# Four gated cross-attention layers on one core: the order of a step's products in layers 0 and 1, and the place of the first experts' additions

## The chip, the cores and the metric

The kernel runs on one core of one Trainium2 chip. The metric is the device time of one execution in microseconds. A core has a tensor engine (PE, with its weight loads listed as PEld), a vector engine (DVE), a scalar engine (ACT), GpSimd (POOL) and a queue engine (SP) that here issues most of the DMAs. Each engine works through its own instructions in order and waits on semaphores for what others make. Matrix products land in PSUM[...].

## What is computed

Input x is 32 batch elements of 100 tokens of width 128; the context has 1444 positions per element. Four layers follow one another, each a gated attention over the context and a gated feed-forward part. The change touches layers 0 and 1:

```python
x = x + tanh(g_xattn[0]) * L0_xattn(layernorm(x), ctx, ctx, ...)   # 16 heads of 8, projections, biases
x = x + tanh(g_ffn[0])   * L0_ffn(layernorm(x), ...)               # shared expert + 8 routed ones, top 2
x = x + tanh(g_xattn[1]) * L1_xattn(ctx, ctx, layernorm(x), mask, W_v, W_o)   # 16 heads, masked by key
x = x + tanh(g_ffn[1])   * L1_ffn(layernorm(x), ...)               # 32 experts, top 4
# layers 2 and 3 follow

def attention_core(q, k, v):                    # of each head
    scores = einsum('bhqd,bhkd->bhqk', q, k) * scale
    return einsum('bhqk,bhkd->bhqd', softmax(scores), v)
```

In the feed-forward part of layer 0 each token's row goes to two experts. Their two results come back weighted and are added to x with the gate of that part. Layer normalization of x stands ahead of each part, so the mean and variance of a token's row are needed after every addition to x.

## The kernel before

**Attention of layers 0 and 1** is `heads_attention` (L273). Layer 1 runs it with `keyed=True`, which the trace shows by its lines (L481, L489, L626 with a bias `kb`). Scores are made twice. By query, queries on the partitions: `query_scores` (L561, product at L574), from three-term bf16 splits of k and q that are laid out over the partitions by a round trip through DRAM (`kd`, `qd`); `query_max` (L586, at L595) takes their maxima on DVE. By key, keys on the partitions: `key_scores` (L551, at L556), from fp32 operands. To these `key_exp` (L605) adds the negative maxima by a product with ones (`oneb`, L611), and ACT takes the exponential out of PSUM (L626 in layer 1, L630 in layer 0). `values` (L633) multiplies the exponentials with the values: three of the four heads of a group at L641, the fourth at L646.

**Steps.** The loop at L785 counts steps g; a batch element takes NT = 12 of them. In one step four row groups c = 0 to 3 of 32 partitions are handled, as the pairs (0, 1) and (2, 3). Three batch elements are in flight: scores by query of element b in steps 12 b to 12 b + 11, scores by key and exponentials `lag` = 14 steps later, values one step after that. Within a step the engines' order is what the code writes down (`manual_schedule`, L784): the entries of `plan` that fall due, then the block at L798 to L818, then `maxima` in the last step of an element, then the entries of `tail` that fall due, then `values(..., False)`. The entries of `tail` make the next elements' keys and queries (`k_part`, `q_in`, `q_out`), the values' projection (`v_part`) and the output (`end_turn`, `end_back`, `end_out`); in layer 1 there is no projection of keys or values. The functions in `beside` add further entries to `tail`.

**Banks.** All PSUM tiles of the attention but the output come from one pool `ps` of seven banks, used in turn (L286, L287); a new tile waits until the readers of the tile that lay seven before it are done. A step takes eight (four `pse`, four `psc`) and one for each product of the tail. The block at L798 takes the two of psc 2 and 3 first, then pse 0 and 1, pse 2 and 3, psc 0 and 1.

**Terms.** `k_seen` (L476, layer 1: keys that the mask hides set to zero), `k_terms` (L491) and `q_terms` (L459) split k and q into bf16 terms. They run on POOL, with a cast by ACT between (`k_first` L484, or the copies in `k_part` and `q_out`). Ahead of step 0 there are 20 steps that prepare element 0 and begin with element 1.

**The experts' results.** At the end of `ffn0` (L1659 to L1671) eight groups of four batch elements are handled in a loop: SP loads y (both results of each token, `back` in DRAM), POOL adds the two (`ya`, L1667), DVE adds the sum with the gate to x (L1669), and `moments` (L190) takes mean and variance of the four rows' sets (L193, L194). Then layer 1's attention begins; it takes the reciprocal deviations of all 32 elements at once with `inv_sqrt` (L196; square root on ACT at L200) and norms an element in the step 13 ahead of its first. Its first loads on SP are the context (L354) and the mask (L356).

Of the kernel before, what the change touches and what calls it, by code (L numbers as in the profile page):

```python
# [16 lines left out]
B, S, D = 32, 100, 128  # L17
# [11 lines left out]
GB = 4  # L29
NG = B // GB  # L30
GT = GB * S
LN_EPS = 1e-5
# [28 lines left out]
class Model:  # L61
# [211 lines left out]
    def heads_attention(self, layer, w, scale, bq=None, bk=None, bv=None, bo=None, keyed=False, beside=()):  # L273
# [7 lines left out]
        nc, tc = self.nc, self.tc  # L281
        E = mybir.EngineType
        with ExitStack() as es:
            pool = lambda n, k, **kw: es.enter_context(tc.tile_pool(name=f"a{layer}_{n}", bufs=k, **kw))
            once, two, three, xp = pool("one", 1), pool("two", 2), pool("three", 3), pool("ex", 3)
            ps, pvp = pool("ps", 7, space=PSUM), pool("pv", 1, space=PSUM)  # L286
            bank = lambda n, dt=F32: ps.tile([P, 512 if dt == F32 else 1024], dt, name=n, tag="s")  # L287
            rstd = self.inv_sqrt(self.mv[:, :, 1], LN_EPS, "ln")
            gate = self.gate_x(layer)

            qm = once.tile([P, NSET, S], F32, name="qm")
# [55 lines left out]
            st = [{} for _ in range(B)]  # L347
# [93 lines left out]
            def q_out(b):  # L441
# [8 lines left out]
                if stacked:  # L450
# [5 lines left out]
                        scale=scale, **bias,  # L456
                    )

            def q_terms(b):  # L459
                r, qt, dram = st[b].pop("qr"), qts[b % 2], self.qd[b % 2]  # L460
                nc.gpsimd.tensor_tensor(r, r, qt[:, 0, 0, :], ALU.subtract)
                nc.gpsimd.tensor_copy(qt[:, 3, 0, :], r)
                nc.gpsimd.tensor_copy(qt[:, 1, 1, :], r)
                nc.gpsimd.tensor_copy(qt[:, 2, 1, :], r)
                nc.gpsimd.tensor_tensor(qt[:, 0, 1, :], r, qt[:, 3, 0, :], ALU.subtract)
                nc.sync.dma_start(
                    dram.rearrange("(p s) n -> p (s n)", s=4), qt.rearrange("p s v q -> p (s v q)")
                )
# [7 lines left out]
            def k_seen(b, i):  # L476

                at = slice(i * QTR, (i + 1) * QTR)
                t = st[b]
                t["kr", i] = two.tile([P, QTR], F32, name="kr")  # L480
                nc.gpsimd.tensor_scalar(t["kr", i], t["mi"][:, at], 0.0, 0.0, ALU.is_equal, ALU.is_equal)  # L481
                nc.gpsimd.tensor_tensor(t["kr", i], t["kr", i], t["k"][:, at], ALU.mult)

            def k_first(b, i):  # L484
                t = st[b]
# [3 lines left out]
                nc.scalar.copy(t["kt", h][:, 0, j * QTR : (j + 1) * QTR], t["kr", i])  # L489

            def k_terms(b, i):  # L491
                t = st[b]
                h, j = divmod(i, 2)
                kt = t["kt", h][:, :, j * QTR : (j + 1) * QTR]
                if keyed:
                    r = k = t.pop(("kr", i))
                else:
                    k = t["k"][:, i * QTR : (i + 1) * QTR]
                    r = two.tile([P, QTR], F32, name="kr")
                nc.gpsimd.tensor_tensor(r, k, kt[:, 0], ALU.subtract)  # L500
                nc.gpsimd.tensor_copy(kt[:, 1], r)
                nc.gpsimd.tensor_tensor(kt[:, 2], r, kt[:, 1], ALU.subtract)  # L502
# [281 lines left out]
            with tc.manual_schedule(engines={E.PE, E.DVE, E.Activation, E.Pool, E.SP}):  # L784
                for g in range(plan[0][0], NT * (B - 1) + end + 5):  # L785
                    def at(step):
                        b, r = divmod(g - step, NT)
                        return b if r == 0 and 0 <= b < B else None

                    for step, f in plan:  # L790
                        if (b := at(step)) is not None:
                            f(b)
                    def now(step):
                        b, t = divmod(g - step, NT)
                        return (b, t) if 0 <= b < B else None

                    keys, queries, products = now(lag), now(0), now(lag + 1)
                    if stacked:  # L798


                        if queries:
                            for c in (2, 3):
                                st[queries[0]]["psc", c] = bank("psc")
                        if keys:
                            key_scores(*keys, (0, 1))
                        if queries:
                            query_scores(*queries, (2, 3))
                            query_max(*queries, (2, 3))
                        if keys:
                            key_scores(*keys, (2, 3))  # L810
                            key_exp(*keys, (0, 1))
                        if queries:
                            query_scores(*queries, (0, 1))
                            query_max(*queries, (0, 1))
                        if keys:
                            key_exp(*keys, (2, 3))
                        if products:
                            values(*products, True)  # L818
                    for cs, others in () if stacked else (((0, 1), (2, 3)), ((2, 3), (0, 1))):
# [677 lines left out]
    def ffn0(self, w):  # L1497
# [4 lines left out]
        with ExitStack() as es:  # L1502
# [153 lines left out]
                    todo = e, i, h, out  # L1656
            down(*todo)

            for g in range(NG):  # L1659
                y = f2.tile([S, GB, K, D], F32, name="y")  # L1660
                i = nc.sync.dma_start(
                    y.rearrange("p b k d -> p b (k d)"),
                    self.back[g * GT * K : (g + 1) * GT * K].rearrange("(b p k) d -> p b (k d)", p=S, k=K),
                )
                self.after(i, back)
                ya = f2.tile([S, GB, D], F32, name="ya")
                nc.gpsimd.tensor_tensor(ya, y[:, :, 0, :], y[:, :, 1, :], ALU.add)  # L1667
                xs = self.x[:, g * GB : (g + 1) * GB, :]
                nc.vector.scalar_tensor_tensor(xs, ya, self.gate_f(0), xs, ALU.mult, ALU.add)  # L1669
                for b in range(g * GB, (g + 1) * GB):  # L1670
                    self.moments(b)  # L1671

    def ffn1(self, w):

# [338 lines left out]
def tile_gated_cross_attention_stack(ctx: ExitStack, tc: tile.TileContext, ins: dict, out: bass.AP):  # L2013
# [22 lines left out]
    with ExitStack() as ctx2:  # L2036
        later = []
        a, f = weights(1, {"q": sq, "t": sq, "o": sq}, {
            "gw": ("F1_gw", [P, 32], None),
            "sel128": ("sel128", [P, 16, P], None, BF16),  # L2040
            "w1": ("F1_w1", [P, 2048], None),
            "w3": ("F1_w3", [P, 2048], None),
            "w2": ("F1_w2", [P, 16, P], None),
            "b2": ("F1_b2", [P, P], None),
            "sw1": ("F1_sw1", sq, None),
            "sw3": ("F1_sw3", sq, None),
            "sw2": ("F1_sw2", sq, None),
        }, later)
        by_query = m.nc.values_load(
            m.by_query[0:1, 0:1], min_val=0, max_val=1, skip_runtime_bounds_check_because="it is a comparison's result"  # L2050
        )
        with tc.If(by_query == 0) as keyed:
            m.heads_attention(1, a, D ** -0.5, keyed=True, beside=[m.loads(later)])
        with keyed.Else():
            m.heads_attention(1, {**a, "k": a["q"], "v": a["q"]}, D ** -0.5, beside=[m.loads(later)])
        m.ffn1(f)
    with ExitStack() as ctx2:
        a, f = weights(2, {"q": sq, "k": sq, "v": sq}, {
# [120 lines left out]
```

## Time and profile before

| | us |
|---|---|
| median of three runs | 4278.3 (4276.38 to 4279.37) |
| the profiled execution, its own time | 4294.4 |
| its span, first to last instruction | 4292.6 |
| busy: PE / DVE / ACT / POOL | 3670.5 / 2845.1 / 2407.5 / 1706.5 |
| mean granted clock of PE | 0.955 |

The stages, from the trace: attention of layer 0 to about 1480, feed-forward of layer 0 to about 1796, a stretch to 1858 in which PE makes nine products in all, attention of layer 1 to about 3205, then the rest.

A row of the time line gives start and length in us, engine, line, operation, output and inputs, partitions x elements, how many instructions were merged, and in brackets how long the engine had been idle and what ended that. A row of a group gives busy time and mean length in ns, then the idle time of the engine ahead of it and who ended most of it. Matmuls overlap: the array works on several row groups at once, and an fp32 product shows as two passes, so each has two rows. Their ends are modelled.

### The profile page before, as it was taken

To read this page: it belongs to the slowest core of one execution; us is meant where nothing else is said; L and a number is where in the kernel's file an instruction comes from. 1 tells how busy PE (TensorE), PEld (TensorE's weight loads), DVE (VectorE), ACT (ScalarE), POOL (GpSimd) and SP (SyncE) were. 2 spreads that over 40 slices of the span, in tenths; PEclk is the share of its full clock that TensorE was granted. 3 is DMA by queue.
4 is the path that set the end of the run, shared out by engine and by line. 5 is a ranking of instruction groups with operands and counts; after the bars stand their busy time and mean duration, and the time that the engine had idled before them with its cause. 6 is when DMAs were issued, how large, how long until landed. Compare 5 with 4: busy or idle time off the path is not lost. (4 is left out here: it accounts for less than half of the span.)

```text
span 4292.6 us, 92353 instructions
## 1 busy us (share of the span) xinstructions
PE 3670.5 (86%) x36522; PEld 1991.4 (46%) x36522; DVE 2845.1 (66%) x6428; ACT 2407.5 (56%) x5274; POOL 1706.5 (40%) x2549
## 2 busy tenths in 40 slices
PE   6999999999999989668888888888887998886587
PEld 2444444444444445424444444444444556764354
DVE  5767767777777643357777777777748875553577
ACT  3666666666666642136666666676662324552474
POOL 5444444444444223465455454544500000113573
PEclk8999999999999989869999999999998999987799
DMA  5354344344343120244443343434310004541331
GB/s 171 126 163 146 119 142 127 106 138 125 112 138 120 61 71 16 71 172 169 150 161 138 139 148 134 162 136 142 134 64 8 1 1 181 199 167 37 115 114 36
DMA packets 286485, 500.06 MB, mean 116 GB/s; under 512 B 54993, under 2 KB 241967, under 8 KB 285258
## 3 DMA queue, kind: packets, MB, share of 16 engines
q1 hardware_dynamic: 275594, 475.26, 33.4%
q0 software_dynamic: 10432, 18.63, 1.4%
q8 instruction: 293, 4.80, 0.5%
q14 instruction: 166, 1.36, 0.1%
HBM read 360.24 MB, written 135.22 MB: 115 GB/s over the span
## 5 line engine op out<-in xcount | busy, mean ns | idle before, releaser
L595 DVE TENSOR_REDUCE mx<-psc 100x1 f32<-100x482 f32 (+1 forms) x3072 | 1824.6, 653 | 741.1 <-PE psc L574 509.4
L574 PE MATMUL psc<-ks,qs 32*100 32x482 bf16 (+1 forms) x6144 | 1184.9, 384 | 335.2 <-DVE mx L595 299.7
L556 PE MATMUL pse<-q,kt 32*128 32x400 f32 x6144 | 1034.5, 527 | 1.0 <-ACT maxt L672 1.0
L626 ACT ACTIVATE ex<-pse,kb 128x400 f32<-128x400 f32 (+1 forms) x1536 | 794.8, 591 | 339.1 <-PE psc L574 137.9
L630 ACT ACTIVATE ex<-pse 128x400 f32<-128x400 f32 (+1 forms) x1536 | 680.8, 502 | 372.9 <-PE pse L611 336.3
L574 PEld LDWEIGHTS <-qs 32*100 32x100 bf16 x6144 | 331.4, 120 | 749.7 <-issue 642.3
L556 PEld LDWEIGHTS pse<-q,kt 32*128 32x128 f32 x6144 | 522.7, 184 | 128.7 <-issue 68.1
L611 PE MATMUL pse<-maxt,oneb 32*128 32x400 bf16 x3072 | 513.8, 334 | 0.2
L661 POOL CAST mexp<-neg 100x16 bf16<-100x16 f32 x64 | 16.2, 253 | 718.7 <-DVE neg L657 454.5
L500 POOL TENSOR_TENSOR kr<-kt,kterm 128x361 f32<-128x361 f32 x128 | 108.3, 846 | 457.1 <-ACT kterm L531 455.3
L641 PE MATMUL pav<-ex,vn 128*32 128x300 f32 (+1 forms) x3072 | 277.2, 429 | 0.7 <-ACT oc L698 0.7
L641 PE MATMUL pav<-ex,v 128*32 128x300 f32 (+1 forms) x3072 | 275.1, 428 | 0.3 <-ACT oc L698 0.3
L502 POOL TENSOR_TENSOR kterm<-kr,kterm 128x361 bf16<-128x361 f32 x256 | 217.3, 849 | 20.7
L500 POOL TENSOR_TENSOR kr<-kr,kterm 128x361 f32<-128x361 f32 x128 | 108.3, 846 | 244.3 <-ACT kterm L489 213.9
L149 POOL DMA_INDIRECT sent<-rows_out,place x96 | 95.5, 995 | 251.6 <-DVE dn L1182 136.5
L1449 ACT ACTIVATE sl<-g,cols 128x400 f32<-128x400 f32 x136 | 80.7, 593 | 202.6 <-PE g L1440 149.8
L251 POOL TENSOR_SCALAR amo<-ami 100x361 bf16<-100x361 int32 x128 | 185.6, 1450 | 13.2 <-DMA ami<-in_mask 13.1
L481 POOL TENSOR_SCALAR kr<-mi 128x361 f32<-128x361 int32 x128 | 184.4, 1440 | 1.8 <-DMA mi<-in_mask 1.8
L611 PEld LDWEIGHTS <-oneb 32*128 32x128 bf16 x3072 | 149.7, 92 | 7.3 <-issue 1.0
L646 PE MATMUL pav<-ex,vn 128*32 128x100 f32 (+1 forms) x3072 | 149.2, 255 | 0.0
L646 PE MATMUL pav<-ex,v 128*32 128x100 f32 (+1 forms) x3072 | 143.5, 258 | 0.0
L522 PE MATMUL pk<-ct,w_A_k 128*128 128x361 f32 x256 | 118.4, 548 | 25.0 <-DMA ct<-in_ctxT 25.0
(491 smaller groups left out, 6011.9 us busy)
## 6 DMA issues: line engine op xcount, KB each, us to landing
ks<-kd SPq DMA_DIRECT2D x128, 722.0 KB
ct<-in_ctxT SPq DMA_DIRECT2D x96, 722.0 KB
kd<-kterm SPq DMA_DIRECT2D x128, 541.5 KB
vn<-in_ctxV SPq DMA_DIRECT2D x32, 1008.0 KB
cnat<-in_ctxN SPq DMA_DIRECT2D x32, 768.0 KB
kd<-kterm SPq DMA_DIRECT2D x128, 180.5 KB
kt<-in_ctxT SPq DMA_DIRECT2D x32, 722.0 KB
mi<-in_mask SPq DMA_DIRECT2D x32, 722.0 KB
```

The lines of the kernel that those rows point to most:

```text
L251: nc.gpsimd.tensor_scalar(t, now[h], 0.0, NEG, ALU.is_equal, ALU.mult)
L481: nc.gpsimd.tensor_scalar(t["kr", i], t["mi"][:, at], 0.0, 0.0, ALU.is_equal, ALU.is_equal)
L500: nc.gpsimd.tensor_tensor(r, k, kt[:, 0], ALU.subtract)
L502: nc.gpsimd.tensor_tensor(kt[:, 2], r, kt[:, 1], ALU.subtract)
L556: nc.tensor.matmul(s_["pse", c][:, : NSET * S], s_["k"][r, t * P : (t + 1) * P], s_["q"][r].rearrange("p s q -> p (s q)"), start=True, sto ...
L574: nc.tensor.matmul(t["psc", c][:S, : z - a], t["qs"][r, s, v, :], t["ks"][r, s, a:z], start=v == 0, stop=v == 1,)
L595: nc.vector.tensor_reduce(mx, src, AX.X, ALU.max)
L611: nc.tensor.matmul(pps[c][:, : NSET * S], oneb[r], s_["max"][r], start=False, stop=not by_query)
L626: nc.scalar.activation(ex[:kp, c], pps[c][:kp, : NSET * S], AF.Exp, bias=s_["kb"][:kp, t : t + 1])
L630: nc.scalar.activation(ex[:kp, c], pps[c][:kp, : NSET * S], AF.Exp)
L641: nc.tensor.matmul(s_["out"][32 * c : 32 * c + 32, S : NSET * S], s_["v"][:kp, t, o + 16 : o + 48], ex[:kp, c, S:], start=t == 0, stop=t = ...
L646: nc.tensor.matmul(s_["out"][32 * c : 32 * c + 32, :S], s_["v"][:kp, t, o : o + 32], ex[:kp, c, :S], start=False, stop=t == NT - 1, skip_g ...
```

## The change

It has three parts.

1. In the block of a step the products with the values (three heads) and the last exponentials now stand ahead of the scores by query of the pair (0, 1) and their maxima. The two banks of psc 2 and 3 are no longer taken first.
2. `ffn0` adds only group 0 of the experts' results. Groups 1 to 7 are loaded and added beside layer 1's attention: loads in steps 1, 5, 9, 13, 17, 21, 25, additions three steps later. The sum on POOL goes; DVE makes two gated additions instead. Layer 1 takes the reciprocal deviations of the first four elements ahead of its loop, and the other 28 in step 30.
3. For batch element 0 of layers 0 and 1 `q_terms`, `k_seen` and `k_terms` run on DVE, not on POOL.

```diff
-            rstd = self.inv_sqrt(self.mv[:, :, 1], LN_EPS, "ln")
+            if layer == 1:
+                rstd = once.tile([S, B], F32, name="rstd")
+                def scales(bs):
+                    v = rstd[:, bs]
+                    nc.vector.tensor_scalar(v, self.mv[:, bs, 1], 1.0, LN_EPS, ALU.mult, ALU.add)
+                    nc.scalar.activation(v, v, AF.Sqrt)
+                    nc.vector.reciprocal(v, v)
+                scales(slice(0, GB))
+                self.rest_of_scales = lambda: scales(slice(GB, B))
+            else:
+                rstd = self.inv_sqrt(self.mv[:, :, 1], LN_EPS, "ln")
...
+            terms_engine = lambda b: nc.gpsimd if b else nc.vector
             def q_terms(b):
-                nc.gpsimd.tensor_tensor(r, r, qt[:, 0, 0, :], ALU.subtract)
+                e = terms_engine(b)
+                e.tensor_tensor(r, r, qt[:, 0, 0, :], ALU.subtract)
...
                     if stacked:
-                        if queries:
-                            for c in (2, 3):
-                                st[queries[0]]["psc", c] = bank("psc")
                         if keys:
                             key_scores(*keys, (0, 1))
                         if queries:
                             query_scores(*queries, (2, 3))
                             query_max(*queries, (2, 3))
                         if keys:
                             key_scores(*keys, (2, 3))
                             key_exp(*keys, (0, 1))
-                        if queries:
-                            query_scores(*queries, (0, 1))
-                            query_max(*queries, (0, 1))
                         if keys:
                             key_exp(*keys, (2, 3))
                         if products:
                             values(*products, True)
+                        if queries:
+                            query_scores(*queries, (0, 1))
+                            query_max(*queries, (0, 1))
...
-            for g in range(NG):
-                y = f2.tile([S, GB, K, D], F32, name="y")
-                i = nc.sync.dma_start(y..., self.back[g * GT * K : (g + 1) * GT * K]...)
-                self.after(i, back)
-                ya = f2.tile([S, GB, D], F32, name="ya")
-                nc.gpsimd.tensor_tensor(ya, y[:, :, 0, :], y[:, :, 1, :], ALU.add)
-                xs = self.x[:, g * GB : (g + 1) * GB, :]
-                nc.vector.scalar_tensor_tensor(xs, ya, self.gate_f(0), xs, ALU.mult, ALU.add)
-                for b in range(g * GB, (g + 1) * GB):
-                    self.moments(b)
+            self.sent_back = back
+            self.results0_add(self.results0(f2, 0), 0)
...
+    def results0_add(self, y, g):
+        xs = self.x[:, g * GB : (g + 1) * GB, :]
+        for k in range(2):
+            self.nc.vector.scalar_tensor_tensor(xs, y[:, :, k, :], self.gate_f(0), xs, ALU.mult, ALU.add)
+        for b in range(g * GB, (g + 1) * GB):
+            self.moments(b)
+
+    def results_beside(self, es):
+        pool = es.enter_context(self.tc.tile_pool(name="cb", bufs=1))
+        now = {}
+        def load(b, i):
+            g = 1 + 3 * b + i
+            if g < NG:
+                now[g] = self.results0(pool, g)
+        def add(b, i):
+            g = 1 + 3 * b + i
+            if g < NG:
+                self.results0_add(now.pop(g), g)
+        def scales(b):
+            if b == 2:
+                self.rest_of_scales()
+        return [(s + d, lambda b, i=i, f=f: f(b, i)) for i, s in enumerate((1, 5, 9))
+                for d, f in ((0, load), (3, add))] + [(6, scales)]
...
-            m.heads_attention(1, a, D ** -0.5, keyed=True, beside=[m.loads(later)])
+            m.heads_attention(1, a, D ** -0.5, keyed=True, beside=[m.results_beside, m.loads(later)])
```

`results0` holds the load that stood in the loop, for one group. The same substitution of `terms_engine` is made in `k_seen` and `k_terms`; the other branch of layer 1 (by query) gets `results_beside` too, and does not run here.

More of the change, by code (lines that the diff above doesn't have):

```diff
@@ L457, in q_out @@
                     )
+            terms_engine = lambda b: nc.gpsimd if b else nc.vector
             def q_terms(b):
                 r, qt, dram = st[b].pop("qr"), qts[b % 2], self.qd[b % 2]
-                nc.gpsimd.tensor_tensor(r, r, qt[:, 0, 0, :], ALU.subtract)
[L462 to L465, printed above, removed]
+                e = terms_engine(b)
+                e.tensor_tensor(r, r, qt[:, 0, 0, :], ALU.subtract)
+                e.tensor_copy(qt[:, 3, 0, :], r)
+                e.tensor_copy(qt[:, 1, 1, :], r)
+                e.tensor_copy(qt[:, 2, 1, :], r)
+                e.tensor_tensor(qt[:, 0, 1, :], r, qt[:, 3, 0, :], ALU.subtract)
                 nc.sync.dma_start(
@@ L478, in k_seen @@
                 at = slice(i * QTR, (i + 1) * QTR)
-                t = st[b]
+                t, e = st[b], terms_engine(b)
                 t["kr", i] = two.tile([P, QTR], F32, name="kr")
-                nc.gpsimd.tensor_scalar(t["kr", i], t["mi"][:, at], 0.0, 0.0, ALU.is_equal, ALU.is_equal)
-                nc.gpsimd.tensor_tensor(t["kr", i], t["kr", i], t["k"][:, at], ALU.mult)
+                e.tensor_scalar(t["kr", i], t["mi"][:, at], 0.0, 0.0, ALU.is_equal, ALU.is_equal)
+                e.tensor_tensor(t["kr", i], t["kr", i], t["k"][:, at], ALU.mult)
             def k_first(b, i):
@@ L491, in k_terms @@
             def k_terms(b, i):
-                t = st[b]
+                t, e = st[b], terms_engine(b)
                 h, j = divmod(i, 2)
@@ L499, in k_terms @@
                     r = two.tile([P, QTR], F32, name="kr")
-                nc.gpsimd.tensor_tensor(r, k, kt[:, 0], ALU.subtract)
-                nc.gpsimd.tensor_copy(kt[:, 1], r)
-                nc.gpsimd.tensor_tensor(kt[:, 2], r, kt[:, 1], ALU.subtract)
+                e.tensor_tensor(r, k, kt[:, 0], ALU.subtract)
+                e.tensor_copy(kt[:, 1], r)
+                e.tensor_tensor(kt[:, 2], r, kt[:, 1], ALU.subtract)
                 if j:
@@ L1657, in ffn0, with results0 @@
             down(*todo)
-            for g in range(NG):
-                y = f2.tile([S, GB, K, D], F32, name="y")
[L1661 to L1664, printed above, removed]
-                self.after(i, back)
-                ya = f2.tile([S, GB, D], F32, name="ya")
-                nc.gpsimd.tensor_tensor(ya, y[:, :, 0, :], y[:, :, 1, :], ALU.add)
-                xs = self.x[:, g * GB : (g + 1) * GB, :]
-                nc.vector.scalar_tensor_tensor(xs, ya, self.gate_f(0), xs, ALU.mult, ALU.add)
-                for b in range(g * GB, (g + 1) * GB):
-                    self.moments(b)
+            self.sent_back = back
+            self.results0_add(self.results0(f2, 0), 0)
+    def results0(self, pool, g):
+        nc, K = self.nc, 2
+        y = pool.tile([S, GB, K, D], F32, name="y")
+        i = nc.sync.dma_start(
+            y.rearrange("p b k d -> p b (k d)"),
+            self.back[g * GT * K : (g + 1) * GT * K].rearrange("(b p k) d -> p b (k d)", p=S, k=K),
+        )
+        self.after(i, self.sent_back)
+        return y
+    def results0_add(self, y, g):
[20 more added lines that the diff above has]
+                for d, f in ((0, load), (3, add))] + [(6, scales)]
     def ffn1(self, w):
@@ L2052, in tile_gated_cross_attention_stack @@
         with tc.If(by_query == 0) as keyed:
-            m.heads_attention(1, a, D ** -0.5, keyed=True, beside=[m.loads(later)])
+            m.heads_attention(1, a, D ** -0.5, keyed=True, beside=[m.results_beside, m.loads(later)])
         with keyed.Else():
-            m.heads_attention(1, {**a, "k": a["q"], "v": a["q"]}, D ** -0.5, beside=[m.loads(later)])
+            m.heads_attention(1, {**a, "k": a["q"], "v": a["q"]}, D ** -0.5, beside=[m.results_beside, m.loads(later)])
         m.ffn1(f)
```

## The prediction

> **What bounds the kernel now.** I read the page's slices and costliest groups first, then the busy time by stage, then single steps in the order of time. Two stages fill most of the span, the attentions of layers 0 and 1:
>
> ```profile
> 84.00:1480.00 1396.00, 1265.93 (x14579) 636.60 (x14573) 993.17 (x1888) 883.43 (x2002) 610.36 (x812) 1.00 0.41 128
> ...
> 1796.00:1858.00 62.00, 2.03 (x9) 1.27 (x13) 18.08 (x80) 3.73 (x11) 39.45 (x53) 0.50 0.50 161
> 1858.00:1890.00 32.00, 31.04 (x147) 10.62 (x147) 30.75 (x56) 3.48 (x12) 19.19 (x31) 0.50 0.57 205
> 1890.00:3205.00 1315.00, 1141.75 (x14956) 575.43 (x14955) 962.00 (x1828) 912.97 (x1965) 620.03 (x941) 0.99 0.40 138
> ```
>
> (Stretch and length, then busy time of PE, PEld, DVE, ACT and POOL, granted clock, DMA share.) In both attentions no engine but PE is near full, and PE's figure counts overlapping row groups, so it is no proof either. The groups name the wait:
>
> ```profile
> L595 DVE TENSOR_REDUCE mx<-psc 100x1 f32<-100x482 f32 (+1 forms) x3072 | 1824.6, 653 | 741.1 <-PE psc L574 509.4
> L574 PE MATMUL psc<-ks,qs 32*100 32x482 bf16 (+1 forms) x6144 | 1184.9, 384 | 335.2 <-DVE mx L595 299.7
> ```
>
> PE waits for the maxima and the maxima for PE. One step of layer 0 with no tail work shows how:
>
> ```profile
> 1022.80 0.60 PE L556 MATMUL pse<-q,kt 32*128 32x400 f32 x2
> 1022.82 0.61 PE L574 MATMUL psc<-ks,qs 32*100 32x480 bf16 x4
> 1023.24 0.52 PE L556 MATMUL pse<-q,kt 32*128 32x400 f32 x4
> 1023.58 0.34 PE L611 MATMUL pse<-maxt,oneb 32*128 32x400 bf16 x2
> 1023.60 0.50 PE L556 MATMUL pse<-q,kt 32*128 32x400 f32 x2
> 1023.75 0.36 PE L574 MATMUL psc<-ks,qs 32*100 32x480 bf16 x1
> 1024.53 0.40 PE L574 MATMUL psc<-ks,qs 32*100 32x480 bf16 x2 [0.42 <-DVE mx L595]
> 1024.54 0.34 PE L611 MATMUL pse<-maxt,oneb 32*128 32x400 bf16 x2
> 1024.73 0.36 PE L574 MATMUL psc<-ks,qs 32*100 32x480 bf16 x1
> 1025.02 0.71 PE L641 MATMUL pav<-ex,v 128*32 128x300 f32 x8
> 1025.55 0.35 PE L646 MATMUL pav<-ex,v 128*32 128x100 f32 x8
> ```
>
> ```profile
> 1023.82 2.37 DVE L595 TENSOR_REDUCE mx<-psc 100x1 f32<-100x480 f32 x4 [1.59 <-PE psc L574]
> 1024.21 1.84 ACT L630 ACTIVATE ex<-pse 128x400 f32<-128x400 f32 x4 [0.59 <-PE pse L611]
> ```
>
> The step is 3.03 us (next one at 1025.83). At 1023.75 one score by query of the pair (0, 1) starts; its partner starts at 1024.53, 0.78 us later, 0.05 after the first maximum is done (1023.82 + 0.66). The cause is the ring of seven banks: a step takes eight, so the eighth, psc 1, gets the bank of this same step's psc 2. The wait stands in every step of both layers (683 in the list of waits). The reader is to see that PE's sequence behind it is late by 0.78 us.
>
> Between the two attentions PE is idle for 62 us:
>
> ```profile
> 1796.14 19.97 SPq L1661 DMA_DIRECT2D y<-back  x8
> ...
> 1823.45 0.36 SPq L356 DMA_DIRECT2D mi<-in_mask  x1
> ...
> 1827.77 1.46 POOL L481 TENSOR_SCALAR kr<-mi 128x361 f32<-128x361 int32 x1 [1.76 <-DMA mi<-in_mask]
> ...
> 1857.92 1.05 PE L574 MATMUL psc<-ks,qs 32*100 32x482 bf16 x8 [26.17 <-DMA qs<-qd]
> ```
>
> Eight loads and additions, then the first mask load (it takes memory the additions free), then POOL's terms.
>
> **Part 1, the new order in a step.** Nothing is added. Let B be the start of the second pair of scores by key (0.44 to 0.46 into a step). From rows of the step above: the product of oneb for pair (2, 3) follows at B + 0.67 (two passes of 0.336), the values 0.25 later (0.167 of streaming, 0.09 until the next shape), and take 0.53. Now psc 0, 1 follow them, second term 0.20 later, then 0.29 to the last values (1024.73 to 1025.02 shows it), then 0.28 to the next step. Here the Trainium skill speaks against the change: "TensorEngine Tiling (Array Packing)", section Tiling Modes, says that changing the tiling mode drains the engine and that different tiles work in parallel. The new order changes mode twice more per step (128x32 values, 32x128 scores, values) and takes psc 0, 1 out of the company of oneb (2, 3). The row for a change: 0.29 from psc to values where 482 columns stream in 0.20, so 0.09; values to a 128x128 product 0.64 against 0.53 without a change, so 0.11. By the rule alone the change costs about 0.2 in each of some 740 steps, near 150 us, plus 0.4 of lost company; by the rows these 0.6 are paid, but the 0.78 of waiting goes. PE alone: psc 0, 1 at B + 0.67 + 0.25 + 0.53 + 0.11 = B + 1.56, next step at B + 2.33.
>
> What is late next are banks of the next step. The eighth bank now comes from the same step's first exponential; that starts 0.95 after B (1024.21 after 1023.25) and ends at B + 1.50 in layer 0, before B + 1.56; with layer 1's 0.59 us exponentials at B + 1.60, 0.05 late. The next second pair takes the banks of the last exponential and of the first maximum of (0, 1). Exponentials, all four now back to back: last one ends at B + 0.95 + 3 x 0.475 + 0.50 + 0.05 = B + 2.93 in layer 0, B + 3.1 in layer 1. Maximum: it starts 0.44 after the second term, as single instructions show (1.73 and 2.17 into a step), ends 0.71 later: B + 1.76 + 1.15 = B + 2.91. So a plain step is 2.93 in layer 0 (3.03 now) and 3.09 in layer 1 (3.10 now).
>
> With tail work of 0.8 us or more on PE these banks are free by then, and the step is 2.33 + tail + 0.45 where it was 3.03 + tail: shorter by 0.25, and by a further 0.1 as the tail no longer pays the change from the values; I take 0.30. The phases of layer 0, twelve to a batch element: six with long tails (pk three times, pv, px with pv, pv with pa) -1.8; three plain -0.3; pk with pm, po -0.1 each; pq with pt 0, as DVE's q, now behind later maxima, holds pq's bank. Sum -2.3 of 45.75 measured; 31 elements: **-71 us**. Layer 1 has short tails: a tail of one bank moves the ring, so both maxima must end (B + 3.49) before the next second pair: px, pm, pa +0.2 together, po -0.1, the long pg -0.3, the short pg +0.3, plain ones -0.3 (one is 3.35 now). Sum -0.2 of 41.4: **-7 us**.
>
> **Part 2, the additions.** Removed from the gap: seven loads, seven POOL sums (1.26), seven DVE additions (0.75). The mask load then waits for group 0 alone: load landed 1800.5, two additions 1.47, so 1802.1 against 1823.45: -21.4. Added beside: seven times two additions of 0.72 and four bnst, mv pairs (1.1), 2.6 us on DVE. Three fall in steps 4, 8, 12, where DVE sets the pace (busy 30.75 of 32): +7.7. Four fall in full steps, behind the maxima; mx of the next step starts up to 2.5 late, and of that some 1.7 passes on: +7. The rest of the scales at step 30: DVE waits in order for ACT's square root with two table loads (1.28 each as at 1892.6): +3, with nothing of its kind in a full step; bounds 0 and 5. The loads on SP stand in front of key reads needed steps later; 0.3 us of issue, hidden. DMA is at 0.40.
>
> **Part 3, first terms on DVE.** In layer 1 POOL's chain is 1827.77 to 1850.5 for four parts and q's terms. DVE on 128x361 from SBUF is not in the trace; nearest row: the addition of 512 columns, 0.75, gives 0.53 by length; the casts lie between 0.2 and 0.5. A part becomes 3.1 with ACT's cast between, for 5.5: 12.4 + 1.9 for norm, q and terms; -8. But DVE is in order, and every part now waits there for ACT with norm behind it; bounds -11 and 0. In layer 0 terms stand ahead of the reciprocal and the norm that PE's third pk waits for (26.46), so the 0.9 saved per part is given back: 0, bounds -2 and +2. Part 2 and 3: -21.4 + 17.7 - 8 = **-12**.
>
> **Sum.** The profiled execution took 4294.4 (span 4292.6): 4294.4 - 71 - 7 - 12 = 4204. The median of the runs shown is 16 lower: **4188**.
>
> **Rivals.** (A) Late maxima. The first maximum of (2, 3) starts 0.75 after its second term (1.01 and 0.26 into a step). I put that down to the scores by key issued earlier and ending at 0.94. If 0.75 is the price from product to DVE, both maxima of (0, 1) end 0.32 later, at the end of the step and in front of the next second pair. Layer 1: +0.19 in five plain steps, +0.32 in six with short tails, 2.9; layer 0: 2.1 by the same count; 155 us over 31 elements: 4188 + 155 = 4343, slower. It decides from 0.44 + 0.32 x 90/155 = 0.62 us on. Against it: the maximum that started 0.44 after its own product. (B) Exponentials bind. Layer 0 gains nothing, as ACT's copies of pk and pv between the exponentials hold banks and the first exponential: 4278 - 19 = 4259. For it: ACT has 883 of 1396 and would be a closed chain in plain steps. Against: long tails leave it over 1 us. (C) Fuller gain: POOL or DVE work falls in the slack and the 0.11 comes back in all tails; layer 0 at -3.1, layer 1 at -1.0: -127 - 12, 4140. That the order doesn't change is excluded: the built program has psc 0, 1 behind the values, waiting on ACT.
>
> **Numbers.** My forecast 0.55 (4150 to 4225), B 0.17, C 0.11, A 0.17. Range 4140 to 4290: it takes in B and C and the near side of A. A measurement of this kernel tells 0.2% (8.6 us) from no change. Faster: 0.55 + 0.11 + 0.12 of B = 0.78, less 0.04 for a forecast that errs as a whole, 0.74; same 0.05; slower 0.21.
>
> **What would show it.** psc 0, 1 without a wait on mx; plain steps of 2.9 in layer 0 and 3.1 in layer 1, long ones 3.7; the maximum of psc 0 0.44 after its product (A wrong) or 0.75; the mask load of layer 1 near 1802 and first scores by query some 29 us sooner relative to the last scatter. Wrong if layer 1's steps exceed 3.3, or the granted clock falls below 0.99 in either attention.

## The result, and the profile after

The changed kernel takes 4303.2 us (median of five, 4296.7 to 4307.0), the kernel before 4279.4 (five, 4276.4 to 4282.2). The ratio is 1.0056, with a 95% interval of 1.0045 to 1.0067: it is slower by 24 us where 90 less were forecast, and lies outside the range. The profiled execution took 4303.2, its span is 4301.4, the mean granted clock 0.956.

Measured from one instruction to another in the two traces, the time went here (us):

| stretch | before | after | difference | forecast |
|---|---|---|---|---|
| start to the first score by query of layer 0 | 43.75 | 46.22 | +2.5 | 0 |
| layer 0, first score by key to last score by query | 1406.9 | 1391.8 | -15.2 | -71 |
| last product of its values to the experts' first product down | 184.0 | 172.1 | -11.8 | 0 |
| last scatter of results to the first score by query of layer 1 | 65.0 | 39.6 | -25.4 | -29.4 |
| from there to its first score by key | 32.0 | 38.1 | +6.1 | +7.7 |
| layer 1, first score by key to last score by query | 1277.2 | 1336.1 | +58.9 | +3 |
| all the rest | 1283.7 | 1277.5 | -6.2 | 0 |

The -11.8 is no gain of the change. The same stretch took 170.4 to 172.8 us in e1 to e8 below and 182.6 to 186.6 in e9 to e12, which ran on another chip. In the trace of before TensorE stops there from 1592 us on, for up to 4.1 us at a time, and its granted clock is 0.91 over 80 us where the changed kernel has 1.00. These 11.8 us are most of the 15 by which that execution lay above its median. So a difference of less than some 10 us between two profiles is used here only where it can be put to an instruction.

The groups of the changed kernel that answer to the two of before:

```profile
L612 DVE TENSOR_REDUCE mx<-psc 100x1 f32<-100x482 f32 (+1 forms) x3072 | 1870.3, 652 | 744.6 <-PE psc L591 682.0
...
L591 PE MATMUL psc<-ks,qs 32*100 32x482 bf16 (+1 forms) x6144 | 1021.9, 390 | 34.8 <-DMA qs<-qd 26.1
```

The wait that the change was read to remove is gone: TensorE's idle time ahead of scores by query fell from 335.2 to 34.8 us. A plain step without a stall (one with no product of the tail) is 2.88 us in both layers, and the maximum of psc 0 starts 0.40 after its second term. Yet the twelve steps of an element are only 0.49 us shorter in layer 0, by their medians, and 1.08 longer in layer 1. This is step 5 of an element of layer 0, where 4.34 us became 5.26 (the time line; the brackets hold the idle time before and what ended it):

```profile
1002.13 0.60 PE L573 MATMUL pse<-q,kt 32*128 32x400 f32 x2
...
1002.23 0.62 DVE L462 SCALAR_TENSOR_TENSOR q<-pq,cols,qm 128x400 f32<-128x400 f32 x1
...
1002.57 0.85 PE L573 MATMUL pse<-q,kt 32*128 32x400 f32 x4
...
1002.89 0.34 ACT L466 ACTIVATE qr<-pq,bqs 128x100 f32<-128x100 f32 x1 [1.38 <-DVE q L462]
...
1003.13 0.50 ACT L467 ACTIVATE qt<-pq,bqs 128x300 bf16<-128x300 f32 x1
...
1003.69 0.60 PE L573 MATMUL pse<-q,kt 32*128 32x400 f32 x1 [0.28 <-ACT qt L467]
```

Read it from the bottom. The fourth score by key starts 1.56 us into the step, where 0.46 is its place; it waits for the bank that pq, a tail product of step 4, had taken. Three readers hold that bank one after the other: VectorE's q, then ScalarE's two copies. VectorE's q was free to start only at 1002.23, behind the last maximum of the pair (0, 1), which now comes at the end of a step. ScalarE, which idled 1.38 us, waited for q. The chain is not new. This is the kernel before, in a step 5 that starts at 1010.92:

```profile
1010.29 0.63 DVE L449 SCALAR_TENSOR_TENSOR q<-pq,cols,qm 128x400 f32<-128x400 f32 x1
...
1010.95 0.34 ACT L453 ACTIVATE qr<-pq,bqs 128x100 f32<-128x100 f32 x1 [0.77 <-DVE q L449]
...
1011.19 0.50 ACT L454 ACTIVATE qt<-pq,bqs 128x300 bf16<-128x300 f32 x1
...
1011.75 0.18 PEld L556 LDWEIGHTS pse<-q,kt 32*128 32x128 f32 x1 [0.18 <-ACT qt L454]
```

There q starts 0.63 us ahead of the step and the copies end 0.77 into it; the fourth score by key waits for them too, until 0.83. Now q starts 0.10 into the step and the copies end at 1.50: both come 0.73 later. In the changed kernel every element shows the wait for q (the view of one line, L466, in both layers):

```profile
L466 ACT ACTIVATE qr<-pq,bqs x32: 343/343/345, 33.1 to 1410.3; 128x100 f32<-128x100 f32 x32
...
  DVE q L462: 46.5, 32
  DVE q L460: 36.8, 32
```

Why ScalarE may not read the bank beside VectorE is told by the Trainium skill, "PSUM — Partial Sum Buffer", section PSUM bank collisions raise a hardware error: two engines in one bank and quadrant at once are an error, reads too, so they are kept in order. The trace shows the order, 64 times of 64, not what happens without it.

In layer 1 step 2 grew from 3.11 to 3.68 us, by late exponentials and by another bank, pm's:

```profile
2422.66 1.06 ACT L643 ACTIVATE ex<-pse,kb 65x400 f32<-65x400 f32 x2
2423.62 0.49 ACT L689 COPY maxt<-pm 128x400 bf16<-128x400 bf16 x1
```

```profile
2423.78 0.56 PE L591 MATMUL psc<-ks,qs 32*100 32x480 bf16 x3
...
2424.18 0.91 PE L573 MATMUL pse<-q,kt 32*128 32x400 f32 x3
```

The step starts at 2422.98. ScalarE ends the exponentials of the step before only at 2423.72, 0.74 into it, and then copies pm until 2424.11. The scores by query of the pair (2, 3) wait for a bank until 0.80, so the third score by key starts at 1.05, where 0.46 is its place. The fourth starts at 1.20: in 29 of the elements its weights are loaded 0.05 us after the copy ends. A count of seven would give it the bank of psc 1, so here the banks are not used strictly in the order in which they were taken.

### The profile page after: what moved, and what is told of

Its sections match the earlier page's. It is cut to its first block, busy times and chain, and to the rows that moved or that the text cites. A ratio compares the mean times of both kernels' runs of the same rounds, so it can differ in the third digit from the quotient of the medians.

```text
span 4301.4 us, 92361 instructions
## 1 busy us (share of the span) xinstructions
PE 3995.8 (93%) x36522; PEld 2039.4 (47%) x36522; DVE 2891.7 (67%) x6480; ACT 2368.0 (55%) x5277; POOL 1670.3 (39%) x2499
## 5 line engine op out<-in xcount | busy, mean ns | idle before, releaser
L612 DVE TENSOR_REDUCE mx<-psc 100x1 f32<-100x482 f32 (+1 forms) x3072 | 1870.3, 652 | 744.6 <-PE psc L591 682.0
L573 PE MATMUL pse<-q,kt 32*128 32x400 f32 x6144 | 1203.3, 537 | 12.3 <-ACT qt L467 8.0
L591 PE MATMUL psc<-ks,qs 32*100 32x482 bf16 (+1 forms) x6144 | 1021.9, 390 | 34.8 <-DMA qs<-qd 26.1
L647 ACT ACTIVATE ex<-pse 128x400 f32<-128x400 f32 (+1 forms) x1536 | 648.6, 508 | 378.8 <-PE pse L628 358.0
L573 PEld LDWEIGHTS pse<-q,kt 32*128 32x128 f32 x6144 | 566.6, 185 | 230.4 <-issue 95.4
L628 PE MATMUL pse<-maxt,oneb 32*128 32x400 bf16 x3072 | 571.2, 332 | 0.2 <-ACT maxt L689 0.2
L591 PEld LDWEIGHTS <-qs 32*100 32x100 bf16 x6144 | 290.0, 120 | 451.5 <-issue 396.4
L628 PEld LDWEIGHTS <-oneb 32*128 32x128 bf16 x3072 | 174.1, 93 | 100.6 <-issue 26.7
L658 PEld LDWEIGHTS pav<-ex,vn 128*32 128x32 f32 (+1 forms) x3072 | 61.9, 108 | 196.9 <-issue 179.5
L658 PEld LDWEIGHTS pav<-ex,v 128*32 128x32 f32 (+1 forms) x3072 | 60.8, 107 | 191.7 <-issue 190.1
```

Of the source, the lines that this page charges most:

```text
L573: nc.tensor.matmul(s_["pse", c][:, : NSET * S], s_["k"][r, t * P : (t + 1) * P], s_["q"][r].rearrange("p s q -> p (s q)"), start=True, sto ...
L591: nc.tensor.matmul(t["psc", c][:S, : z - a], t["qs"][r, s, v, :], t["ks"][r, s, a:z], start=v == 0, stop=v == 1,)
L612: nc.vector.tensor_reduce(mx, src, AX.X, ALU.max)
L628: nc.tensor.matmul(pps[c][:, : NSET * S], oneb[r], s_["max"][r], start=False, stop=not by_query)
L647: nc.scalar.activation(ex[:kp, c], pps[c][:kp, : NSET * S], AF.Exp)
L658: nc.tensor.matmul(s_["out"][32 * c : 32 * c + 32, S : NSET * S], s_["v"][:kp, t, o + 16 : o + 48], ex[:kp, c, S:], start=t == 0, stop=t = ...
```

## The experiments

Each was timed in four to eleven runs beside the kernel before. They ran on three chips, and the kernel before took 4275.9 us beside e1 to e4, 4275.6 beside e5 to e8, and 4291.1 beside e9 to e12. "To before" is the difference on the same chip; the last column is the ratio with its 95% interval. The times that were expected of e9 to e12 count from the earlier chips, so 15 us are to be added to them.

| kernel | us | to before | ratio |
|---|---|---|---|
| e1 new order alone | 4298.3 | +22.4 | 1.0057 (1.0043 to 1.0071) |
| e2 all but the new order | 4277.8 | +1.9 | 1.0007 (0.9998 to 1.0016) |
| e3 new order in layer 0 only | 4263.7 | -12.2 | 0.9970 (0.9961 to 0.9979) |
| e4 changed kernel, q from a copy | 4238.5 | -37.4 | 0.9912 (0.9897 to 0.9927) |
| e5 e4, old order in layer 1 | 4231.5 | -44.1 | 0.9900 (0.9885 to 0.9915) |
| e6 e4, pm a step sooner | 4390.8 | +115.1 | 1.0271 (1.0257 to 1.0285) |
| e7 e4, additions spread | 4238.1 | -37.6 | 0.9913 (0.9900 to 0.9927) |
| e8 e4, first terms on GpSimd | 4246.6 | -29.1 | 0.9935 (0.9922 to 0.9949) |
| e9 e6, pm ahead of the casts | 4246.4 | -44.7 | 0.9898 (0.9883 to 0.9913) |
| e10 e9, additions spread, layer 0's terms on GpSimd | 4240.3 | -50.8 | 0.9881 (0.9866 to 0.9896) |
| e11 e4, no additions beside | 4252.4 | -38.7 | 0.9907 (0.9894 to 0.9921) |
| e12 e9, no additions beside, layer 0's terms on GpSimd | 4238.2 | -52.9 | 0.9876 (0.9861 to 0.9891) |

**e1 and e2: the two halves.** e1 is the kernel before with the last hunk in the step; e2 the changed kernel without it.

```diff
--- e1, against the kernel before
-                        if queries:
-                            for c in (2, 3):
-                                st[queries[0]]["psc", c] = bank("psc")
...
-                        if queries:
-                            query_scores(*queries, (0, 1))
-                            query_max(*queries, (0, 1))
...
                             values(*products, True)
+                        if queries:
+                            query_scores(*queries, (0, 1))
+                            query_max(*queries, (0, 1))
```

> The kernel before with the new order of a step alone (no additions beside, no first terms on VectorE). Theory 1 (the order itself is the loss: in layer 1 the second pair of scores by key now waits for banks that late maxima and the copies behind them hold, q's in step 5 and the maxima's copy in step 2): layer 0 some 15 us shorter, layer 1 some 45 us longer than before, so 4279 + 30 = 4309, range 4295 to 4325. Rival 2 (the order is worth what was forecast, 78 us, and the additions on VectorE beside layer 1 push every maximum late): 4200 to 4225.

> The changed kernel with the old order of a step: additions beside the second attention and first terms on VectorE alone. Theory 1: gap between the attentions 25 shorter, the start of layer 1's steps 6 longer, start of layer 0 2.5 longer, the seven additions some 8 longer, so 10 us faster than before: 4269, range 4260 to 4278. Rival 2 (the additions beside are the loss in layer 1's steps, 59 us): 4310 to 4330.

The order costs 22.4 us by itself and the rest gains nothing that can be measured. In e1's trace layer 0's steps are the 15.4 us shorter and layer 1's 37.3 longer; in e2's, layer 1's are 21.3 longer in the old order. So layer 1's +58.9 has two causes, and both rivals, that one half does it all, fall. e2 came out at the upper end of its range, for the additions cost 21 us and not 8.

**e3: the order by layer.** Layer 0 keeps the new order, layer 1 has the old one.

```diff
+                        new = layer == 0
+                        if new:
+                            if keys:
+                                key_scores(*keys, (0, 1))
...
+                        else:
+                            if queries:
+                                for c in (2, 3):
+                                    st[queries[0]]["psc", c] = bank("psc")
...
```

> The changed kernel with the new order in layer 0 only; layer 1 keeps the old one. Theory 1: the 15 us of layer 0 stay gained and layer 1's 50 are not lost: 4303 - 50 = 4253, range 4243 to 4268. Rival 2: layer 1's loss stays because the additions cause it: 4300 to 4315.

As theory 1 has it: 12.2 us faster than before, with the order worth 14 in layer 0 (against e2) and costing 36 in layer 1 (against the changed kernel's +23.8).

**e4: q's bank.**

```diff
+                if stacked:
...
+                    qr = st[b]["qr"] = two.tile([P, S], F32, name="qr")
+                    nc.scalar.activation(qr, pq[:, :S], AF.Identity, scale=scale, **bias)
+                    nc.scalar.copy(qts[b % 2][:, :3, 0, :], qr.unsqueeze(1).to_broadcast([P, 3, S]))
+                    spread = qr.unsqueeze(1).to_broadcast([P, NSET, S])
+                    nc.vector.tensor_tensor(st[b]["q"], spread, qm, ALU.mult)
+                    return
...
-                    nc.scalar.activation(
-                        qts[b % 2][:, :3, 0, :], pq[:, :S].unsqueeze(1).to_broadcast([P, 3, S]), AF.Identity,
-                        scale=scale, **bias,
-                    )
```

Layers 0 and 1 return here, ahead of VectorE's product that read pq. The mask qm holds no scale, since the copy has it already.

> The changed kernel with q's bank released sooner: ScalarE copies pq once, and its second copy and VectorE's q read that copy instead of the bank. Theory 1 (pq's bank, held to 1.5 us into step 5, costs 1.1 us per batch element in layer 0 and 0.85 in layer 1): step 5 back to 4.2 in layer 0 and 3.4 in layer 1, 62 us in all: 4241, range 4230 to 4262. Rival 3 (the late maxima of the pair (0, 1) hold the banks behind it, so the wait moves to the next bank): less than 20 us, 4285 to 4303.

One bank, released sooner, moves 61 us (from +23.8 to -37.4). The time line of e4 around a step 5, which starts at 980.37:

```profile
979.73 0.34 ACT L462 ACTIVATE qr<-pq,bqs 128x100 f32<-128x100 f32 x1
980.11 0.44 ACT L463 CAST qt<-qr 128x300 bf16<-128x300 f32 x1
...
980.37 0.60 PE L574 MATMUL pse<-q,kt 32*128 32x400 f32 x2
...
980.81 0.52 PE L574 MATMUL pse<-q,kt 32*128 32x400 f32 x4
```

The bank is free at 980.07, before the step begins, and all of the second pair is under way from 980.81. Step 5 is 4.05 us in layer 0 and 3.11 in layer 1. Rival 3, that the next bank takes the wait over, is excluded: all other steps kept their lengths within 0.05. That the copy is worth something in the old order as well is excluded in layer 1 by e5, where step 5 is 3.48 as in the kernel before; in layer 0 no run has the copy with the old order.

**e5: is the new order worth having in layer 1 once q is mended?** e4 with the switch of e3.

> The kernel of e4 (q from the copy) with the old order in layer 1. Theory 1 (with q's bank free, layer 0 is worth 49 us and layer 1's new order still loses in the steps with short tails): e4 and e3 together, 4238 - 15 = 4223, range 4214 to 4232. Rival 3 (once q's bank is free the new order is worth having in layer 1 as well): 4240 to 4255.

The old order stays better there, by 7 us in the medians, half of what was expected and near what they can tell. In the traces layer 1 is 14.4 us longer in e4: 7.1 in the first two elements, beside the additions, and 7.3 in the other thirty. Without the additions, too, the new order with q mended is 7.1 us longer there than the old one (e11 against the kernel before, 1284.3 and 1277.2), some 0.2 in almost every element. By the median steps, step 2 pays 0.57 and steps 5 and 9 gain 0.37 and 0.23. Their sums for an element, 41.49 and 41.47, would make the orders even; so small a difference is not seen in them.

**e6, a miss: pm one step sooner.**

```diff
-            tail += [(NT + 1, maxima_t)]
+            tail += [(NT if keyed else NT + 1, maxima_t)]
```

> The kernel of e4 with the turn of the maxima (pm and its copy) one step sooner in layer 1. Theory 1 (step 2 of layer 1 is 0.6 us long because the copy of pm stands on ScalarE behind late exponentials, its product and its bank with it): step 2 back from 3.68 to 3.2, the step before it some 0.1 longer, 31 elements: 12 us faster than e4, 4226, range 4220 to 4234. Rival 4 (late exponentials and maxima alone set these steps, and the wait moves with pm): within 4 us of e4, 4234 to 4243.

It is 152 us slower than e4. ScalarE's part of step 1, which begins at 2478.56, in the time line:

```profile
2478.59 0.26 ACT L453 COPY xt<-px 128x100 f32<-128x100 f32 x1
2480.18 0.49 ACT L507 CAST kterm<-kr 128x361 bf16<-128x361 f32 x1 [1.32 <-POOL kr L500]
2480.57 0.49 ACT L690 COPY maxt<-pm 128x400 bf16<-128x400 bf16 x1
```

The copy of pm now stands behind a cast that waits for GpSimd, so its bank comes free 2.5 us into the step, and TensorE's next score by key starts at 2481.11. What follows is dearer than the stop. The busy time by stretch (stretch and length, then PE, PEld, DVE, ACT and POOL, the granted clock, DMA share, GB/s):

```profile
2475.00:2480.00 5.00, 5.00 (x55) 2.25 (x51) 3.87 (x8) 2.75 (x7) 3.27 (x7) 1.00 0.01 3
2480.00:2485.00 5.00, 3.89 (x31) 1.26 (x34) 1.52 (x4) 2.92 (x6) 4.16 (x6) 0.72 0.19 72
2485.00:2490.00 5.00, 5.00 (x36) 1.70 (x34) 2.19 (x5) 2.43 (x5) 0.56 (x2) 0.50 0.61 183
2490.00:2495.00 5.00, 5.00 (x40) 1.93 (x36) 2.17 (x5) 2.54 (x5) 4.37 (x5) 0.50 0.82 336
```

Behind TensorE's stop of 1.1 us (by its modelled ends) the granted clock is 0.50 for some 17 us, and the steps after it are 5.27 us long. The Trainium skill, "TensorE: Matmul & The Clock Gate", section Part 1, gives about 3.4 us of idling for this; here less was enough. Elements 2 to 30 all have such a stop (1.05 to 1.14 us, once 1.47). Behind 25 of the 29 the granted clock fell, for 3.4 to 17.1 us. Behind four it did not, and there (at 2435.71, for one) the stop cost only itself, 5.10 us and then 3.15. What decides between the two is not shown.

**e9: the same move, ahead of the cast.**

```diff
-            tail += [(NT if keyed else NT + 1, maxima_t)]
+            tail = [(NT, maxima_t)] + tail if keyed else tail + [(NT + 1, maxima_t)]
```

> The kernel of e6 with the turn of the maxima and its copy at the head of the tail in layer 1, so that ScalarE's copy of pm stands ahead of the cast of the key terms, which in e6 waited for GpSimd until 1.64 us into step 1. Theory 1 (pm's bank costs step 2 its 0.6 us, and e6 failed by what the copy stood behind): step 2 at 3.15, step 1 at 3.5 to 3.7 and no fall of the clock, so 12 to 15 us faster than e4: 4225, range 4217 to 4231. Rival 4 (any place of pm one step sooner loses, since late exponentials decide): 4236 or more.

Step 2 is 3.36 (3.68 in e4), step 1 3.20 (3.51), step 0, which now has pm beside px, 3.66 (3.39): with the rest 0.33 less in an element, 10 us in 31. Step 1 came out better than expected and step 2 worse (3.15). By the ratios e9 is 6 us faster than e4, which they hardly tell; e12 against e11, on one chip, differs by this and layer 0's terms and is 14 us faster. The sum of the median steps, 41.16, is what was forecast for layer 1 (41.2). Without the additions, layer 1 takes 1272.8 us (e12), 4.4 less than in the kernel before. Rival 4 falls.

**e7, e11: the additions beside the second attention.** e7 adds one element a step, with a load each, out of six buffers where there was one; e11 puts the additions ahead of the attention, as before.

```diff
-        return [(s + d, lambda b, i=i, f=f: f(b, i)) for i, s in enumerate((1, 5, 9))
-                for d, f in ((0, load), (3, add))] + [(6, scales)]
+        return [(1 + i + d, lambda b, i=i, f=f: f(b, i)) for i in range(12)
+                for d, f in ((0, load), (3, add))] + [(8, scales)]
```

> The kernel of e4 with the additions beside layer 1 spread, one batch element a step with its own load, instead of four elements in every fourth step. Theory 1 (3.1 us of additions ahead of both maxima stop TensorE for 2.8 us, and the granted clock then falls to 0.5 for two steps, so one group costs 4 to 6 us where it holds VectorE 3): no stop over 1 us, clock stays 1.00, the four groups in full steps cost 2 us each instead of 5: 12 us faster than e4, 4226, range 4220 to 4234. Rival 5 (the additions cost their VectorE time wherever they stand): within 4 us of e4, 4234 to 4243.

> The kernel of e4 with the first experts' results added ahead of the second attention, as before (part 2 undone). Theory 1 (the gap is 21 us shorter by part 2, but the steps beside the additions take 27 us for it): the gap 21 us longer, layer 1 some 25 to 28 shorter, 4 to 7 us faster than e4: 4232, range 4226 to 4238. Rival 7 (part 2 gains the 4 us of the forecast's sum, 21.4 less 17.7): 4240 to 4246.

The mechanism was seen in e2, which has the old order. VectorE and TensorE in its time line, then the same time by stretch:

```profile
1878.87 1.53 DVE L1693 SCALAR_TENSOR_TENSOR x<-y,tg,x 100x512 f32<-100x512 f32 x2
...
1882.04 1.19 DVE L612 TENSOR_REDUCE mx<-psc 100x1 f32<-100x480 f32 x2
...
1882.72 0.64 PE L591 MATMUL psc<-ks,qs 32*100 32x480 bf16 x2 [2.76 <-DVE mx L612]
```

```profile
1878.00:1882.00 4.00, 1.96 (x25) 1.21 (x26) 3.79 (x12) 2.48 (x6) 1.85 (x3) 1.00 0.21 85
1882.00:1886.00 4.00, 3.28 (x31) 1.61 (x34) 2.45 (x5) 1.08 (x2) 3.92 (x8) 0.53 0.62 201
1886.00:1890.00 4.00, 3.86 (x34) 1.24 (x26) 2.45 (x4) 2.16 (x4) 1.02 (x2) 0.50 0.84 257
```

One group holds VectorE from 1878.87 to 1882.04, 3.2 us; TensorE stops for 2.76; then the clock halves, and the next steps take 4.95 and 3.87 us instead of 3.11. Four groups and the scales make the first nineteen steps 21.4 us longer than in the kernel before (92.1 against 70.6).

Spread, the additions let these steps go at a clock of 0.89 instead of 0.73 and in 81.1 us instead of the 96.0 of e4, and cost 3.8 more ahead of them. But the medians of e7 and e4 are alike, as rival 5 has it. The profiled execution of e4 lay 4 us above its median, that of e7 3 below; that explains 7 of the 11 us, and what is left is less than the medians tell. So that the clock falls behind a block of additions is shown (behind each of the four groups in e2, once for 3.4 us in e7); what spreading them is worth is not settled, between nothing and 10 us. Part 2 as a whole is no gain: in e11 the gap is 21.3 us longer, the way to the first score by key 6.8 and the steps 25.5 shorter; e11 and e4 do not differ by their ratios.

**e8: the first terms.**

```diff
-            terms_engine = lambda b: nc.gpsimd if b else nc.vector
+            terms_engine = lambda b: nc.gpsimd
```

> The kernel of e4 with the first element's terms back on GpSimd in both layers. Theory 1 (part 3 saves the gap of layer 1 what its own rows show, VectorE's 13.6 us from first mask to last term against GpSimd's 22.7, less the 5 us that SP's loads stand behind, and costs layer 0 2.5): layer 0's first scores 2.5 us sooner, layer 1's 4 to 9 later, so 2 to 7 us slower than e4: 4243, range 4239 to 4247. Rival 6 (part 3 gains nothing, since the loads behind the terms end last): 4233 to 4238.

By the medians it is 8 us slower than e4, with intervals that overlap a little. The trace puts 3.5 us less to layer 0's start and 4.4 more to the gap, 0.9 together; the other 7 are not located, so what part 3 is worth as a whole stays open. That VectorE's terms gain in layer 1 and lose in layer 0 is read from the two places.

**e10 and e12: the parts that gained, together.** Both have e4's copy, e9's place for pm, and the first terms on VectorE in layer 1 alone; e10 spreads the additions, e12 does not have them beside.

> The kernel of e9 with the additions spread as in e7, and layer 0's first terms back on GpSimd. Theory 1: e9 less some 8 for the additions (11 by the profiles of e4 and e7, nothing by their medians) and less 3 for layer 0's start: 4214, range 4207 to 4226. Rival 5 (the additions cost the same wherever they stand): e9 less 3.

> The kernel of e9 with part 2 undone as in e11, and layer 0's first terms back on GpSimd. Theory 1: e9 less 5 less 3: 4217, range 4209 to 4226. Rival 7 (part 2 is worth having): slower than e10 by 4 or more.

Both beat the kernel before, by 1.2%, and do not differ from each other by their intervals, so rival 7 falls. Against e9 they gain 6 and 8 us, where 11 and 8 were expected.

## Why the prediction failed

**TensorE's own sequence: right.** The wait on the maximum went. Psc 0 starts 1.57 us behind the second pair of scores by key (1.56 forecast), so the drain of which the Trainium skill warns ("TensorEngine Tiling (Array Packing)", section Tiling Modes) cost what the rows had said. A plain step of layer 0 is 2.88 us (2.93 forecast). The first maximum starts 0.40 after its product (0.44), so rival A's price of 0.75 is wrong: A came nearer with its 4343, but not by its cause. Rival B gave layer 0 no gain; it gained 15.2. Two of the prediction's own signs of being wrong came true: the plain step 2 of layer 1 exceeds 3.3, and the granted clock in that attention is 0.98.

**"pq with pt 0, as DVE's q, now behind later maxima, holds pq's bank": the step that failed.** It saw the bank and counted q alone. ScalarE's two copies stand behind q in the same bank, 0.84 us more in layer 0, and the fourth score by key of step 5 waits for the last of them. The sum had 0 for this step and -0.30 for the next ("pv with pa"). Steps 4 and 5 came to -0.29 and +0.92, so +0.63 where -0.30 was forecast. In layer 1 the sum had no term for it, and step 5 is +0.60. e4 shows the cause: with the bank released sooner, both are gone, 61 us.

**Layer 1's "px, pm, pa +0.2 together".** The term let the pair behind such a tail wait for the two maxima. Behind pm it waits for late exponentials and then for ScalarE's copy of pm: +0.57 in step 2. e9 gives 0.32 of it back, which is pm's bank; the other half stays, by the trace behind the exponentials. Steps 5 and 2 together, 1.17 us in 31 elements, are about as much as the 37 us that e1's layer 1 lost. Of the plain steps, step 9 gained 0.20, and 3, 7 and 11 lost 0.04 to 0.11.

**Layer 0's long tails, "0.30 each".** Right for px with pv and, in e4, for pv with pa (-0.29 each); half of it for pv (-0.14); wrong for the three pk steps (3, 7 and 11), -0.13, +0.07 and +0.08. Steps 1, 4 and 6 gained 0.29 each, more than their 0.1, 0 and 0.1, and the plain step 2 lost 0.18. In the trace the fourth score by key starts 0.05 late in steps 3 and 11 and 0.22 in step 7, behind the late maxima of the pair (0, 1), and the products with the values 0.15 and 0.33; no run took this apart. Of the 1.8 us by which an element of layer 0 fell short, q's bank is 0.93; most of the rest lies in the pk steps, and its cause is argued only. With q mended an element of layer 0 takes 44.05 us, where 43.45 was forecast.

**The additions: the price.** 7 us for four groups, with 1.7 passed on from each, were 21 with the scales: VectorE is held 3.2 us where 2.6 were counted, and the clock was left out. The scales, put at 3, are not the cause: the step behind them (31) is 0.5 longer in e2. The three groups ahead of the full steps cost 6.1 (7.7).

**The gap: right in its first half.** The first mask load follows the last scatter by 9.2 us instead of 30.6, the 21.4 that was forecast. Terms on VectorE took 13.6 us instead of 22.7, but q's terms now come last and the loads behind them end 5 later: -4.0 instead of -8. In layer 0 they cost 2.5 to 3.5, above the bound of 2.

**Sum.** The order was put at -78 and is +22 (e1); the rest at -12 and is +2 (e2). With both banks released sooner the order gains some 47 by the medians (e9 against e2). By the traces of e12 and of the kernel before, layer 0 is then 47.8 us shorter (71 forecast) and layer 1 4.4 (7).

## What to carry to other kernels

When products move to the end of a step, list for every bank of the ring all readers in the order in which the program makes them wait, on each engine's own queue: a copy that cost nothing behind one engine holds the bank through the next step when its partner comes late. Read a tail product from its bank once and make the other forms from that copy. A block of work on the engine that TensorE waits for may cost twice, its own length and the clock behind it; that shorter blocks are worth their place was not shown here (e7).

## What was not expected of the hardware

The granted clock fell to 0.50 behind stops of 2.76 us (e2) and behind most stops of 1.1 us (e6), and stayed there for 3.4 to 17.1 us; a step of layer 1 is then 5.27 us instead of some 3.2. The mask comparisons, casts, products and differences of 128x361 on VectorE take 0.34 to 0.54 us where GpSimd takes 0.48 to 1.46, by the profile's rows.
